# Two token tiles in a bank of PSUM: the output products of the GLUs and of layer 1's heads, added to the residual in one operation per pair

## The chip, the cores and the metric

The kernel runs on one core of a Trainium2 chip, as one program in one launch. A core has engines with instruction queues of their own: TensorE for matmuls (PE in the profile; PEld is its loading of weights), VectorE (DVE), ScalarE (ACT), GpSimd (POOL), and SyncE (SP), which here only issues DMAs. They wait for one another through semaphores. SBUF is the working memory of 128 partitions; PSUM holds results of matmuls. The metric is the device time of one execution in microseconds, the median of several runs.

## The reference

A residual stream x of 2048 tokens (4 sequences of 512) by 256 columns in fp32 goes through four layers. In each, a mixer and a feed-forward part read the same layernorm of x, and both are added to x:

```python
xn = layernorm(x)                  # before each layer
x = x + mixer(xn) + ffn(xn)

# the gated linear unit (GLU), in all four layers' feed-forward parts
y = (silu(xn @ w_gate) * (xn @ w_up)) @ w_down

# layer 0: mixer = Mamba2, 32 heads of 64, state 128, causal convolution of 4; ffn = GLU(1024)
# layer 1: mixer = latent attention, 16 heads, causal, rotary; ffn = GLU(1024) + 8 of 512 product-key experts
out = softmax(mask(qf @ kf.T * scale)) @ v          # per head
mixer = out.reshape(b, s, 16 * 128) @ wo
# layer 2: mixer = attention over heads within a token; ffn = top 2 of 8 experts (width 128) + a shared GLU(256)
# layer 3: mixer = causal attention, 16 heads of 128;   ffn = top-p weighted GLUs of 8 experts (width 512)
```

What the change touches is the last product of a GLU and of layer 1's heads, and the addition of these products to x.

## The kernel before

x lives in SBUF as `c.x`: 128 partitions by 16 token tiles by 256 columns (`DM`), four tiles (`TPB`) to a sequence, four sequences (`NB`). The normalized x stands transposed in `c.xnT`. Weights arrive in units by DMA.

**PSUM** has eight banks of 512 fp32 columns, given out by `c.ps(tag)`: four of tag "mm", two of "tr", two of "acc". A tile of a tag takes the bank whose last reader has finished. "tr" serves transposes above all, "acc" sums of output products.

**A GLU** (`glu_pieces`, L163-L211) takes a unit of weights and goes through the sequences. For each of its `n` column blocks of 128 it makes gate and up projections for 512 tokens (L134, in `project`), the activation (`sg`, L195, or `silu_times`) and their product hT (L196). Then, tile by tile, it multiplies the hT blocks by the output weights: `n` matmuls (L203) into the first half of a bank, 256 columns; `add_scaled` (L147) adds that half bank to x with one VectorE instruction, `tensor_add` at L151, or with a factor per token (layer 3's experts) `scalar_tensor_tensor` at L152. Layer 0's GLU and a quarter of layer 1's (the first of two units, for sequences 0 and 1) run beside Mamba, with output in "tr" banks and five hT buffers; the remaining layer 1 pieces run beside the heads and product-key experts in "acc" banks. Layer 2's shared GLU has two blocks of 128, layer 1's and layer 0's units have four.

**Layer 1's heads** (`latent_pieces`) go through 4 groups of 4 heads, 4 sequences and 2 pairs of heads. Scores (L631) become probabilities (L634 on VectorE, exponent on ScalarE), are transposed (L812, "tr"), and multiplied with the compressed values (L856, "acc") into `zT` (L862). After the second pair, the output products of the four token tiles follow at L869: two matmuls to a half bank of "acc", added to x by `add_scaled`. Queries with the rotary part come from L787 to L789 (`psw`, `qf`) and from L899 and L902 (`qT`). Layer 3's heads have their own output loop (`heads_out`, L647), which calls `add_scaled` too.

**Order of work.** Each of these functions is a generator; `weave` (L214) runs several together. After each `yield` the stream that is least far along by its share of cost goes on, and the number yielded is what it has then spent. `weave` also counts down `c.later`: the transposes of a sequence's layernorm wait for eight such steps, or until a stream needs that sequence (`c.settle`). `c.part_done(b)` says that one contribution to a sequence of x is complete, and starts the next layernorm with the last one. From this program order a scheduler makes the queue of each engine; it can move an instruction ahead where its buffers and inputs allow, unless `keep_in_program_order` pins it. [...]

**Mamba** (layer 0) projects, convolves (L268, `xc` at L272), transposes `xc` (L415, "tr") into `xdt` (L417), makes decays by a scan (L409, POOL L435) and state updates (`S`, L464 to L470), adds the partial `y` (POOL L458, VectorE L479), and multiplies it with the output weights group by group (L495, "tr"); each product is copied to or added to `acc` in SBUF (ScalarE L499, VectorE L501), which frees the bank, and `acc` goes to x at L514.

**Layer 2's experts** sort the tokens into slots per half of the sequences. `dispatch` (router scores L1290, `chosen` L1275, positions `at` L1340, normalized weights `tot` L1374) gives `ids`; `gather` (L1383) fetches the rows of each slot from the normalized x in DRAM by an indirect DMA, issued by POOL, two tiles to a pair of slots, into `xs`: three buffers for the first half of the sequences, one for each pair for the second. Then `experts` goes through the pairs: transposes (`turn`, L1401), projections (`hidden`, L1413; hs at L1421), transposes (`turn_hidden`, L1427), output (`down`, L1435, copied at L1440). Beside it runs `head_mix`, whose projections are at L142 and L1171, with `prod` on POOL at L1188 and the addition to x on VectorE at L1193.

```python
weave(c, (shared, 41.0, 0.0), (dispatch(), 34.0, 0.0), flush=False)
weave(
    c, (experts[0], 40.0, 0.0), (mix(), 12.0, 0.0),
    (last.gather(xs, len(PAIRS), every), 12.0, 0.0), flush=False,
)
```

Of the kernel before, what the change touches and what calls it, by code (L numbers as in the profile page):

```python
# [15 lines left out]
P = 128  # L16
NB, SEQ, DM = 4, 512, 256
NT = NB * SEQ
NTILE = NT // P
TPB = SEQ // P  # L20
# [62 lines left out]
def v3(ap, b):  # L83
    return ap.rearrange("p (a b) -> p a b", b=b)
# [46 lines left out]
def project(c, out, w, cols, tokens):  # L131

    for d in range(2):
        c.nc.tensor.matmul(  # L134
            out, lhsT=w[:, d, cols], rhs=c.xnT[:, d, tokens], start=(d == 0), stop=(d == 1)
        )
# [10 lines left out]
def add_scaled(c, t, part, w=None):  # L147

    x = c.x[:, t, :]
    if w is None:  # L150
        return c.nc.vector.tensor_add(x, part, x)  # L151
    return c.nc.vector.scalar_tensor_tensor(x, part, w, x, ALU.mult, ALU.add)  # L152


def silu_times(c, pool, out, gate, other):


    sg = c.tile(pool, [P, SEQ], "sg", bufs=2)
    c.nc.scalar.activation(sg, gate, AF.Tanh, scale=0.5)
    c.nc.vector.scalar_tensor_tensor(sg, sg, 1.0, gate, ALU.add, ALU.mult)  # L160
    c.nc.vector.scalar_tensor_tensor(out, sg, 0.5, other, ALU.mult, ALU.mult)


def glu_pieces(
    c, pool, srcs, n=4, width=512, split=1, factor=None, tanh=False, bufs=8, out_tag="acc",
    last=True, first=0, loaded=False, seqs=range(NB),
):

    nc = c.nc
    per = n // split
    for u, src in enumerate(srcs, first):
        w = src if loaded else c.unit(src)
        wg = v3(w[:, : 2 * width], width)
        wu = v3(w[:, 2 * width : 4 * width], width)
        wd = v3(w[:, 4 * width : 4 * width + n * DM], DM)
        for b in seqs:  # L180
            tokens = slice(b * SEQ, (b + 1) * SEQ)
            c.settle(b)
            hT = []
            for k in range(n):
                cols = slice(k * P, (k + 1) * P)
                pg, pu = c.ps(), c.ps()
                project(c, pg, wg, cols, tokens)
                project(c, pu, wu, cols, tokens)
                h = c.tile(pool, [P, SEQ], "hT", bufs=bufs)
                hT.append(h)  # L190
                if tanh:
                    silu_times(c, pool, h, pg, pu)
                else:
                    sg = c.tile(pool, [P, SEQ], "sg", bufs=2)
                    nc.scalar.activation(sg, pg, AF.Silu)  # L195
                    nc.vector.tensor_mul(h, sg, pu)  # L196
                yield 3.4
            for t in range(TPB):
                for s in range(split):
                    po = c.ps(out_tag)[:, :DM]  # L200
                    for i in range(per):
                        k = s * per + i
                        nc.tensor.matmul(  # L203
                            po, lhsT=hT[k][:, t * P : (t + 1) * P], rhs=wd[:, k, :],
                            start=(i == 0), stop=(i == per - 1),
                        )
                    tt = b * TPB + t
                    add_scaled(c, tt, po, factor(u * split + s, tt) if factor else None)
                if last and u == first + len(srcs) - 1 and t == TPB - 1:
                    c.part_done(b)  # L210
                yield 0.43 * n  # L211


def weave(c, *streams, flush=True):  # L214
# [442 lines left out]
def latent_pieces(c, a, keep, prep, open_pool):  # L657
# [4 lines left out]
    nc, tc = c.nc, c.tc  # L662
# [13 lines left out]
    with prep as pre:  # L676
# [3 lines left out]
        for b in range(NB):  # L680
# [3 lines left out]
            for t in range(TPB):  # L684
                tt = b * TPB + t
# [98 lines left out]
    def rotate(pes, psw, qf):  # L784
        pec = c.tile(pool, [P, SEQ], "pec", bufs=1)
        nc.vector.tensor_mul(pec, pes, cosq)
        tc.keep_in_program_order(nc.vector.tensor_mul(psw, psw, sinq))  # L787
        nc.vector.tensor_add(qf[:KL, 1, :], pec[:KL, :], psw[:KL, :])
        nc.vector.tensor_add(qf[KL:, 0, :], pec[KL:, :], psw[KL:, :])  # L789

    def probabilities(s, i):
        p, h = s // 2, s % 2
        b = p // 2 % 4
        if i == 0:
            totals[s] = c.tile(pool, [P, TPB], "total")
        rinv = totals[s]
        prs[s].append(exp_scores(
            c, pool, late, qfs[p][:, h, :], kf[:, h, b * SEQ : (b + 1) * SEQ], i, rinv[:, i : i + 1]
        ))
        if i >= TPB - 2:  # L800

            done = slice(0, i + 1) if i < TPB - 1 else slice(i, i + 1)
            nc.vector.reciprocal(rinv[:, done], rinv[:, done])
            for j in range(TPB)[done]:
                nc.scalar.mul(prs[s][j], prs[s][j], rinv[:, j : j + 1])  # L805

    def turned(s, j):

        pt = c.ps("tr")
        n = SEQ - j * P  # L810
        for i in range(j, TPB):
            nc.tensor.transpose(  # L812
                pt[:, (i - j) * P : (i - j + 1) * P], prs[s][i][:, j * P : (j + 1) * P], c.ident
            )
        copy = nc.scalar.copy if j % 2 else nc.vector.tensor_copy
        return lambda: copy(PTs[s][:, START[j] : START[j] + n], pt[:, :n])

    START = (0, 512, 896, 1152)
    qfs, prs, totals, PTs, zTs = {}, {}, {}, {}, {}
# [3 lines left out]
    for s in range(65):  # L823
        if s < 64:
            prs[s] = []
        for i in range(TPB):
            if s < 64:
                probabilities(s, i)
            if s > 0:
                if i == 0:  # L830
                    PTs[s - 1] = c.tile(pool, [P, 1280], "PT")
                ready, copy = copy, turned(s - 1, i)
                if ready:
                    ready()
            if i == 0 and s % 2 == 1 and s < 63:
                rotate(*turning)
            yield 0.85
            if i == 1 and s % 2 == 0 and s < 62:
                turning = queries(s // 2 + 1)
                yield 2.6  # L840
        if copy:
            copy()
            copy = None
        if s > 0:
            del prs[s - 1]
        if s % 2 == 1:
            continue
        if s == 0:
            continue

        p = s // 2 - 1
        g, b, pair = p // 8, p // 2 % 4, p % 2
        z = c.ps("acc")
        for j in range(TPB):
            for h in range(2):
                tc.keep_in_program_order(nc.tensor.matmul(  # L856
                    z[h * KL : (h + 1) * KL, j * P :], lhsT=cv[:, b * TPB + j, :],
                    rhs=PTs[s - 2 + h][:, START[j] : START[j] + SEQ - j * P],
                    start=(j == 0), stop=(j == TPB - 1),
                ))  # L860
        zTs[pair] = c.tile(pool, [P, SEQ], "zT", bufs=3)
        nc.scalar.copy(zTs[pair], z)  # L862
        yield 2.1
        if pair == 1:
            wz = weights[g][4]
            for t in range(TPB):
                po = c.ps("acc")[:, :DM]
                for k in range(2):
                    nc.tensor.matmul(  # L869
                        po, lhsT=zTs[k][:, t * P : (t + 1) * P], rhs=wz[:, k, :],  # L870
                        start=(k == 0), stop=(k == 1),
                    )
                add_scaled(c, b * TPB + t, po)
                if g == 3 and t == TPB - 1:
                    c.part_done(b)
                yield 0.85


def product_key_pieces(c, a, keep, pool, dram, xn):
# [901 lines left out]
```

## Time and profile before

| what | value |
|---|---|
| median of 3 runs (lowest to highest) | 3194.76 us (3190.83 to 3198.62) |
| the profiled execution | 3179.26 us |
| its span in the trace | 3177.5 us |
| granted TensorE clock, mean | 0.992 |
| DMA packets moved | 185.16 MB, mean 58 GB/s |

The profiled execution is one run, with the time of each instruction. Its own time lies 1.8 us above its span, and 15.5 us below the median of the timed runs. The page gives for each engine its busy time, its share of the span and its number of instructions. In the rows of groups stand line, engine, operation, output and inputs, shape and number; then busy time and mean duration in ns; then the idle time of the engine just ahead of them, with what ended most of it. The waits list, for one engine, which line waited for which tile of which engine, the total in us, how often, and the longest. A line of the timeline has start and duration in us, engine, line, operation, and in brackets the idle time before it with its releaser. The layers follow one another: layer 0 runs to about 903 us of the span, layer 1 to 1530, layer 2 to 1800, layer 3 to the end, with some work of a layer beside the end of the one before it.

### The profile page before, as it was taken

What the parts mean: (1) busy time and instruction counts of PE and PEld (TensorE: products, weight loads), DVE (VectorE), ACT (ScalarE), POOL (GpSimd) and SP (SyncE); (2) the same over time, 40 slices, a digit from 0 to 9 for tenths busy, and PEclk for the clock granted to TensorE, in tenths of its full rate; (3) what the DMA queues carried; (4) which work ended last, traced back from release to release, by engine and by line L of the source; (5) the groups of instructions that cost most, each with busy time, mean ns of one, the idle gap of its engine ahead of it and who ended that gap; (6) DMA issues with size and microseconds to landing.
All of it is one profiled execution on the core that took longest, in us unless ns stands there. A gap on an engine that the chain in (4) does not pass through costs nothing.

```text
span 3177.5 us, 35877 instructions
## 1 busy us (share of the span) xinstructions
PE 3081.6 (97%) x12502; PEld 1879.8 (59%) x12502; DVE 1851.9 (58%) x4786; ACT 1257.6 (40%) x2908; POOL 640.0 (20%) x525
## 2 busy tenths in 40 slices
PE   8999999999899999999989999999999999999999
PEld 5566566565555555555566566566666665555555
DVE  5777778777677777887646654554554522222222
ACT  4434435444356666667424433333333401111111
POOL 0464545555400122331053000000000000000000
PEclk9999999999899999999999999999999999999999
DMA  4233233232310244344143000000000000000000
GB/s 130 77 103 119 93 95 110 89 117 83 110 36 25 68 98 116 103 112 142 47 113 110 7 21 7 1 27 1 21 1 1 20 20 20 20 20 20 0 0 27
DMA packets 89091, 185.16 MB, mean 58 GB/s; under 512 B 14192, under 2 KB 57216, under 8 KB 84176
## 3 DMA queue, kind: packets, MB, share of 16 engines
q1 hardware_dynamic: 74448, 135.05, 13.1%
q0 software_dynamic: 14176, 47.01, 6.1%
q8 instruction: 99, 1.62, 0.2%
q10 hardware_dynamic: 288, 0.82, 0.1%
q14 instruction: 80, 0.66, 0.1%
HBM read 160.95 MB, written 12.98 MB: 55 GB/s over the span
## 4 chain that ended last, share of the span: by engine, by line
PE 78%; DVE 10%; DMA 4%; POOL 3%; ACT 2%; issue 2%; SPq 1%; DVEq 0%; ACTq 0%; POOLq 0%
PE mm L134 31%; PE acc L203 8%; PE mm L631 7%; PE mm L142 5%; PE acc L1102 4%; PE acc L647 3%; DMA G<-own 2%; PE tr L1094 2%; PE tr L495 2%; DVE G L409 2%; DVE cy L268 2%; PE tr L812 2%; PE acc L856 1%; PE acc L869 1%; DMA psw<-pes 1%
## 5 line engine op out<-in xcount | busy, mean ns | idle before, releaser
L134 PE MATMUL mm<-xnT,wu 128*128 128x512 f32 x2128 | 955.6, 596 | 2.3 <-ACT sg L195 0.7
L134 PEld LDWEIGHTS mm<-xnT,wu 128*128 128x128 f32 x2128 | 398.4, 191 | 461.3 <-issue 430.8
L638 ACT ACTIVATE pr<-pr,nm 128x128 f32<-128x128 f32 (+3 forms) x512 | 285.9, 559 | 294.3 <-DVE nm L634 292.8
L195 ACT ACTIVATE sg<-mm 128x512 f32<-128x512 f32 x176 | 104.6, 594 | 607.0 <-PE mm L134 606.9
L196 DVE TENSOR_TENSOR hT<-sg,mm 128x512 f32<-128x512 f32 x176 | 120.4, 684 | 380.7 <-PE mm L134 369.0
L634 DVE CUSTOM_DVE_ANT_0 pr<-mm,late 128x128 f32<-128x128 f32 (+3 forms) x512 | 245.0, 482 | 88.3 <-PE mm L631 82.4
L203 PE MATMUL acc<-wu,hT 128*128 128x256 f32 x1280 | 290.9, 380 | 0.7 <-DVE x L151 0.4
L203 PEld LDWEIGHTS acc<-wu,hT 128*128 128x128 f32 x1280 | 240.0, 190 | 51.3 <-issue 19.2
L134 PE MATMUL mm<-xnT,w_in 128*128 128x512 f32 x512 | 231.1, 596 | 0.4 <-DVE hT L196 0.4
L973 POOL DMA_INDIRECT e<-in_p_experts,ids x128 | 128.4, 1003 | 451.7 <-DVE x L152 366.0
L409 DVE TENSOR_TENSOR_SCAN G<-G,eye 128x1024 f32<-128x1024 f32 x64 | 157.0, 2453 | 52.3 <-DMA G<-own 51.8
L631 PE MATMUL mm<-kf,qf 128*128 128x128 f32 (+3 forms) x512 | 179.1, 446 | 7.9 <-DVE qf L789 5.7
L435 POOL TENSOR_TENSOR G<-G,CB 128x1024 f32<-128x1024 f32 x64 | 151.8, 2372 | 162.0 <-DVE G L409 80.5
L268 DVE SCALAR_TENSOR_TENSOR cy<-mm,ws,cy 128x511 f32<-128x511 f32 (+2 forms) x216 | 158.7, 741 | 41.4 <-ACT cy L264 37.8
L631 PE MATMUL mm<-k,q 128*128 128x128 f32 (+3 forms) x512 | 176.6, 435 | 1.1 <-DVE q L1067 1.1
L421 ACT ACTIVATE xD<-xc,ws 128x128 f32<-128x128 f32 x256 | 84.8, 391 | 203.9 <-POOL y L458 191.6
L134 PEld LDWEIGHTS mm<-xnT,w_in 128*128 128x128 f32 x512 | 97.1, 192 | 101.3 <-issue 94.3
L152 DVE SCALAR_TENSOR_TENSOR x<-acc,cw,x 128x256 f32<-128x256 f32 x128 | 61.9, 483 | 155.5 <-PE acc L203 155.5
L1102 PE MATMUL acc<-PT,V 128*128 128x512 f32 (+3 forms) x512 | 149.5, 433 | 0.0
L1067 DVE TENSOR_SCALAR q<-mm,bias 128x512 f32<-128x512 f32 x64 | 48.0, 750 | 169.1 <-PE mm L134 169.1
L151 DVE TENSOR_TENSOR x<-acc,x 128x256 f32<-128x256 f32 x168 | 70.5, 421 | 118.4 <-PE acc L647 98.4
L812 PEld LDWEIGHTS tr<-con,pr 128*128 128x128 f32 x640 | 81.7, 143 | 90.2 <-ACT pr L805 28.8
(308 smaller groups left out, 5017.8 us busy)
## 6 DMA issues: line engine op xcount, KB each, us to landing
G<-own SPq DMA_DIRECT2D x64, 512.0 KB, 4.3
w_in<-in_m_units SPq DMA_DIRECT2D x16, 1024.0 KB, 5.2
eb<-since SPq DMA_DIRECT2D x96, 128.0 KB, 3.2
wu<-in_o_units SPq DMA_DIRECT2D x8, 1536.0 KB, 6.5
wo<-in_m_units SPq DMA_DIRECT2D x16, 512.0 KB, 3.8
psw<-pes SPq DMA_DIRECT2D x128, 64.0 KB, 2.6
wu<-in_g_units SPq DMA_DIRECT2D x4, 1536.0 KB, 6.8
wu<-in_f_units SPq DMA_DIRECT2D x4, 1536.0 KB, 6.9
```

The source lines that it names most:

```text
L134: c.nc.tensor.matmul(out, lhsT=w[:, d, cols], rhs=c.xnT[:, d, tokens], start=(d == 0), stop=(d == 1))
L142: c.nc.tensor.matmul(out, lhsT=c.xnT[:, d, tokens], rhs=w[:, d, cols], start=(d == 0), stop=(d == 1))
L203: nc.tensor.matmul(po, lhsT=hT[k][:, t * P : (t + 1) * P], rhs=wd[:, k, :], start=(i == 0), stop=(i == per - 1),)
L268: nc.vector.scalar_tensor_tensor(y[:, j:], src[:, : SEQ - j], conv[:, k, 3 - j : 4 - j], y[:, j:], ALU.mult, ALU.add,)
L409: nc.vector.tensor_tensor_scan(flat, flat, eye.rearrange("p h t -> p (h t)"), 0.0, ALU.mult, ALU.add)
L435: nc.gpsimd.tensor_mul(G, G, seqs[b][2][:, t, :][:, None, :].to_broadcast([P, HG, P]))
L631: nc.tensor.matmul(sc, lhsT=q[:, i * P : n], rhs=k[:, :n], start=True, stop=True)
L634: nc.vector.tensor_tensor_reduce(out=pr, in0=sc, in1=late[:, SEQ - n :], scale=1.0, scalar=-NEG, op0=ALU.add, op1=ALU.min, accum_out=nm,)
L638: nc.scalar.activation(pr, pr, AF.Exp, bias=nm, scale=-1.0, accum_out=total)
L812: nc.tensor.transpose(pt[:, (i - j) * P : (i - j + 1) * P], prs[s][i][:, j * P : (j + 1) * P], c.ident)
L973: nc.gpsimd.indirect_dma_start(out=e, out_offset=None, in_=a["p_experts"], in_offset=bass.IndirectOffsetOnAxis(ap=ids[:, t, k : k + 1], ax ...
L1102: nc.tensor.matmul(z[:, j * P :], lhsT=head["V"][:, j, h, :], rhs=head["PT"][:, j, j * P :], start=(j == 0), stop=(j == TPB - 1),)
```

## The change

A new function `add_pair` adds 512 columns, two neighbouring token tiles, to x in one `tensor_add`. `glu_pieces` without a factor now takes two tiles at a time: 2 x `n` matmuls fill the two halves of one bank, one addition follows, and the yield carries the cost of both tiles. With a factor (layer 3's experts) it goes tile by tile as before. The output loop of layer 1's heads does the same, with 4 matmuls to a bank. Layer 3's heads keep `add_scaled`. The matmuls themselves, their shapes and number, are the same.

```diff
+def add_pair(c, t, parts):
+
+    x = c.x[:, t : t + 2, :]
+    c.nc.vector.tensor_add(x, parts, x)
...
-            for t in range(TPB):
+
+            step = 1 if factor else 2
+            for t in range(0, TPB, step):
                 for s in range(split):
-                    po = c.ps(out_tag)[:, :DM]
-                    for i in range(per):
-                        k = s * per + i
-                        nc.tensor.matmul(
-                            po, lhsT=hT[k][:, t * P : (t + 1) * P], rhs=wd[:, k, :],
-                            start=(i == 0), stop=(i == per - 1),
-                        )
+                    po = v3(c.ps(out_tag)[:, : step * DM], DM)
+                    for j in range(step):
+                        for i in range(per):
+                            k = s * per + i
+                            nc.tensor.matmul(
+                                po[:, j, :], lhsT=hT[k][:, (t + j) * P : (t + j + 1) * P],
+                                rhs=wd[:, k, :], start=(i == 0), stop=(i == per - 1),
+                            )
                     tt = b * TPB + t
-                    add_scaled(c, tt, po, factor(u * split + s, tt) if factor else None)
-                if last and u == first + len(srcs) - 1 and t == TPB - 1:
+                    if factor:
+                        add_scaled(c, tt, po[:, 0, :], factor(u * split + s, tt))
+                    else:
+                        add_pair(c, tt, po)
+                if last and u == first + len(srcs) - 1 and t == TPB - step:
                     c.part_done(b)
-                yield 0.43 * n
+                yield 0.43 * n * step
...
-            for t in range(TPB):
-                po = c.ps("acc")[:, :DM]
-                for k in range(2):
-                    nc.tensor.matmul(
-                        po, lhsT=zTs[k][:, t * P : (t + 1) * P], rhs=wz[:, k, :],
-                        start=(k == 0), stop=(k == 1),
-                    )
-                add_scaled(c, b * TPB + t, po)
-                if g == 3 and t == TPB - 1:
+            for t in range(0, TPB, 2):
+                po = v3(c.ps("acc"), DM)
+                for j in range(2):
+                    for k in range(2):
+                        nc.tensor.matmul(
+                            po[:, j, :], lhsT=zTs[k][:, (t + j) * P : (t + j + 1) * P],
+                            rhs=wz[:, k, :], start=(k == 0), stop=(k == 1),
+                        )
+                add_pair(c, b * TPB + t, po)
+                if g == 3 and t == TPB - 2:
                     c.part_done(b)
-                yield 0.85
+                yield 1.7
```

## The prediction, made before any run of the changed kernel

> **What bounds the kernel now.** I read first the page's busy times, then a table of four stages (the four layers, cut where their first projections begin), then what PE waited for, then the rows of the touched operations.
>
> ```profile
> PE 3081.6 (97%) x12502; PEld 1879.8 (59%) x12502; DVE 1851.9 (58%) x4786; ACT 1257.6 (40%) x2908; POOL 640.0 (20%) x525
> 0.00:903.00 903.00, 854.40 (x3971) 531.49 (x3972) 674.05 (x1003) 395.15 (x837) 419.61 (x305) 0.99 0.32 101
> 903.00:1530.00 627.00, 603.67 (x2634) 344.68 (x2635) 483.77 (x1693) 407.83 (x1086) 121.72 (x122) 0.99 0.34 89
> 1530.00:1800.00 270.00, 249.34 (x1130) 175.58 (x1127) 167.97 (x521) 107.36 (x217) 87.06 (x82) 0.97 0.26 75
> 1800.00:3178.00 1378.00, 1374.24 (x4773) 828.02 (x4770) 526.10 (x1569) 347.26 (x770) 11.62 (x16) 1.00 0.04 13
> ```
>
> The stage lines give length, then busy us of PE, PEld, DVE, ACT and POOL, granted clock, DMA share, GB/s. PE is the bound everywhere: its idle time is 48.6, 23.3, 20.7 and 3.8 us, 96 us in all. DVE is busy 75% of layer 0 and 77% of layer 1, so a shorter DVE queue pays only where PE waits for it. Those waits (line waited for, us in total, times, longest):
>
> ```profile
> PE tr L1401 <- DMA xs<-xn_half,ids: 11.7, 1, 11.7
> PE tr L415 <- DVE x L151: 6.1, 6, 3.7
> PE acc L869 <- DVE x L151: 3.6, 1, 3.6
> PE tr L495 <- DVE x L151: 3.3, 3, 1.7
> PE tr L203 <- DVE acc L501: 2.7, 2, 2.1
> PE mm L1290 <- DVE chosen L1275: 2.5, 1, 2.5
> PE tr L495 <- DVE acc L501: 2.3, 2, 2.0
> PE acc L203 <- DVE x L151: 0.4, 1, 0.4
> ```
>
> L151 is the addition that the change pairs; PE waits 13.4 us for it (6.1 + 3.6 + 3.3 + 0.4), always to get a PSUM bank back. L501 frees the same two "tr" banks: 5.5 us more (2.7 + 2.3, and 0.5 at L415, not shown). The rows of the operations:
>
> ```profile
> L151 DVE TENSOR_TENSOR x<-acc,x 128x256 f32<-128x256 f32 x168 | 70.5, 421 | 118.4 <-PE acc L647 98.4 <-PE acc L203 11.2 <-PE acc L869 8.1
> L151 DVE TENSOR_TENSOR x<-tr,x 128x256 f32<-128x256 f32 x40 | 16.6, 414 | 4.3 <-PE tr L203 4.3
> L470 DVE TENSOR_TENSOR S<-mm,S 128x512 f32<-128x512 f32 x32 | 22.1, 690 | 3.2 <-PE mm L464 0.4
> ```
>
> The last is what the change makes: a 128x512 fp32 addition of PSUM to SBUF. The others add half as much.
>
> [...] a pair fills it with separate 256-column matmuls, so the bank count stays and each matmul keeps its 380 ns row. [...] 5-us windows after stalls of 3.72, 3.30 and 11.66 us show granted clocks of 0.71, 0.50 and 0.50. After the longest, one group of four transposes takes 1.20 us where 0.60 is usual. I price a slow phase at 1.8 us[...].
>
> **The change, part by part.**
>
> *DVE.* Of the 208 L151 additions, 144 pair up: 40 on tr (32 of layer 0's GLU, 8 of layer 1's), 64 of layer 1's heads (L869) and 24 of its GLU on acc, 16 of layer 2's shared GLU. 144 x 0.421 = 60.6 us become 72 x 0.690 = 49.7 us: 11 us less, on an engine that isn't the bound, hence nothing directly. Layer 3's 64 heads additions and its expert GLU (L152) keep their form.
>
> *PE.* The same matmuls, nothing direct. But the order of the built instructions changes: 60 groups of four L203 matmuls become 30 groups of eight. A bank is held for 8 matmuls, and one is needed half as often. I counted in PE's order how much matmul work, by trace durations, lies between the last matmul into a bank and the first of its next use. On tr, reuses with under 1.8 us of cover fall from 15 to 4; those of L415 after L203, which carry the 3.72 us stall, from 6 to 0. On acc, 15 reuses of L869 after L869 with under 1 us don't exist any more. Layer 3's order is unchanged.
>
> *Layer 0.* The tr waits that can go: 6.1 + 3.3 + 5.5 = 14.9 us, plus 1.8 of slow clock = 16.7. Their cause is often DVE's queue: before the 3.72 us stall, the addition sat behind y (L479), which waited for POOL. A PE that gets past the bank meets the next result of the same queue. Bounds: all kept, -16.7; none, 0. I take rather under half, -7.
>
> *Layer 1.* L869's 3.57 us came from an addition behind psw (L787), which waited 4.89 us for a DMA. With 3.6 + 0.4 and a slow phase, 5.8 us can go; closeness of probabilities to their transposes (L812) also improves, with under 1 us of cover 11 times before and 3 after. Against that, L902's eight matmuls stand 0.35 us nearer to qT on average (2.8 us if all surface) and one L203 directly follows its hT (at most some 1.5 us). From -7 to +4; I take -4.
>
> *Layer 2.* The 16 additions of the shared GLU fall where the queues of a gather decide. Before, POOL's order is the first half's gathers for pairs 0 to 3 (of expert slots), all 23 of the second half, then pairs 4 to 7, then prod (L1188). Each takes 1.25 us. PE stalls at pair 4:
>
> ```profile
> 1631.47 1.20 PE L1401 MATMUL tr<-con,xs 128*128 128x128 f32 x4 [11.66 <-DMA xs<-xn_half,ids]
> 1637.42 1.94 POOL L1188 TENSOR_TENSOR prod<-s,qkv 128x1024 f32<-128x1024 f32 x1
> 1639.39 1.22 DVE L1193 TENSOR_TENSOR x<-x,prod 128x1024 f32<-128x1024 f32 x1 [3.96 <-POOL prod L1188]
> 1641.40 0.38 PE L1427 MATMUL tr<-con,hs 128*128 128x128 f32 x2
> ```
>
> After, L1401's transposes of pairs 0 to 2 stand ahead of the last L203 groups, so their buffers come free earlier and gathers of pairs 4 and 5 go ahead of the 23. Pair 4's stall goes. Late next is prod, still behind 23 + 4 gathers on POOL; L1193 waits for it, and on DVE the hs of pair 4 stands behind L1193. The 23 start at 1596.2 instead of 1598.3, since ids come some 2 us earlier (the 2.5 us wait for chosen is covered by moved work), end at 1625, two more pairs' gathers at 1630, prod at 1632, L1193 at 1633.3, hs at 1633.7. PE, without its stall and that wait, is there at about 1624.7 and waits 9 us. The pair-4 transpose at 1641.4 comes at about 1633.8: 7.6 us gained, less some 2 us for a slow clock that now follows. I take -5. Bounds: -14 if prod slips in between the gathers and no new stall forms (11.7 + 2.5), +1 if the new one costs as much as the old ones. POOL's descriptor queue is where I trust the arithmetic least: gathers took 3.2 us in the median from issue to landing[...].
>
> *Larger pieces.* A yield hands over to another stream: two tiles are now one piece of 8 x 0.38 = 3.0 us before another stream has its turn, and layernorm's transposes, due after eight steps, come later by work. Price 0 where the table of covers is right.
>
> Sum: -7 - 4 - 5 + 0 = -16 us on the profiled execution's 3179.26 us (span 3177.5 and 1.8 around it): 3163. The shown median is 15.5 us above that execution; shifted by the same 16, it becomes **3179 us**, 0.995 of before.
>
> **Rivals.**
>
> *No change.* Waits only move: in layers 0 and 1 the next DVE result is late by as much, and prod's wait takes the whole place of the gather's. For it: layer 0's DVE is itself chained to POOL and to DMA. Against: the covers of data, not only of banks, are equal or better. It gives -3 to 0: 3193.
>
> *More.* All bank waits go (16.7 + 5.8) and layer 2 keeps its 5: -27.5, 3167. For it: DVE is also relieved of 11 us of work, most of it in these two layers. Against: PE's idle time in layers 0 and 1 is 72 us, most of it with other causes; a PE that is early meets these.
>
> *Slower.* Lumps starve the chains that the output tiles filled. The covered waits sit in Mamba's scan and in the heads; each was filled by single 1.5 us groups, and now every second filler is missing there. 64 pairs lie in layers 0 to 2 outside the shared GLU; if a third of them each cost one missing filler of 1.5 us, that is 21 x 1.5 = +32 us, with the -16: +16, 3211. It decides once more than eleven pairs lose one filler each. Against: in the built order other streams' work has moved into those gaps.
>
> **How the numbers follow.** Chances: forecast 0.52, more 0.16, no change 0.17, slower 0.15. A measurement tells about 0.2% from none, 6.4 us. The forecast's own range is 3172 to 3188, of which nearly all is faster; "more" reaches to 3163, slower up to 3215. From 3164 to 3196 holds about eight in ten: it leaves out most of "slower". Faster: 0.16 + 0.52 with little taken off, plus a little of "no change": 0.69. Same: 0.16. Slower: 0.15.
>
> **What would show it.** Right: L151 left with 64 instructions; 72 additions of 128x512 at about 0.69 us; PE waits for "x" on tr and acc under 5 us in all; the second stage's idle about 4 us less and the first's about 7; no wait at L1401 for xs near 1620, but one of about 9 us at L1427 or what feeds it, with prod as its end; layer 3 within 1 us. Wrong: new waits of PE, each 1 to 2 us, in layers 0 and 1 for xc, xdt, hT, PT or qf, which would be the starving; a granted clock below 0.99 there; or an idle sum in layer 2 above 21 us.

## The result, and the profile after

| | before | changed |
|---|---|---|
| median of 22 runs each, us | 3191.36 | 3182.81 |
| lowest to highest | 3181.78 to 3200.39 | 3170.12 to 3192.93 |
| ratio, 95% interval | | 0.9972 (0.9962 to 0.9983) |
| the profiled execution | 3179.26 | 3176.93 |

The change gains 0.28%, 8.5 us by the medians, where 16 were forecast. The two profiled executions lie only 2.3 us apart, since that of before was faster than all 22 timed runs of its kernel (12.1 us below their median; that of the changed kernel 5.9 below). One run of a later experiment took 5384.6 us at a granted clock of 0.554; the ratios leave it out. The page's line of busy times and the four stages of the changed kernel:

```profile
PE 3091.7 (97%) x12502; PEld 1890.4 (60%) x12502; DVE 1847.0 (58%) x4714; ACT 1259.5 (40%) x2910; POOL 636.4 (20%) x525
0.00:903.00 903.00, 858.39 (x3993) 537.57 (x3994) 677.72 (x991) 395.64 (x839) 415.95 (x305) 0.98 0.32 101
903.00:1530.00 627.00, 610.39 (x2678) 350.17 (x2677) 479.43 (x1659) 412.36 (x1098) 121.40 (x122) 0.99 0.33 88
1530.00:1800.00 270.00, 251.07 (x1072) 175.98 (x1071) 164.78 (x498) 104.35 (x204) 87.40 (x82) 0.94 0.26 75
1800.00:3175.00 1375.00, 1371.90 (x4764) 826.71 (x4762) 525.06 (x1567) 347.18 (x770) 11.61 (x16) 1.00 0.04 13
```

PE is busy 10.1 us longer (3091.7 against 3081.6) with the same 12502 instructions, and the granted clock of the third stage fell from 0.97 to 0.94. PE idles 12.4 us less (83.5 against 95.9 us), and matmuls at a slower clock take most of that back. To see where, one needs marks that are the same work in both kernels: the first and last scores matmul of layer 1's heads, and the first of layer 3's. The lines of one source in each kernel (before first), with first and last start:

```profile
L631 PE MATMUL mm<-kf,qf x512: 272/486/634, 909.9 to 1524.0; 128*128 128x128 f32 x43, 128*128 128x256 f32 x43, 128*128 128x512 f32 x43, 128*128 128x384 f32 x42
L631 PE MATMUL mm<-k,q x512: 272/474/676, 1727.3 to 2531.6; 128*128 128x128 f32 x43, 128*128 128x256 f32 x43, 128*128 128x512 f32 x43, 128*128 128x384 f32 x42
```

```profile
L643 PE MATMUL mm<-kf,qf x512: 272/484/697, 902.2 to 1513.0; 128*128 128x128 f32 x43, 128*128 128x256 f32 x43, 128*128 128x512 f32 x43, 128*128 128x384 f32 x42
L643 PE MATMUL mm<-k,q x512: 272/474/676, 1725.2 to 2529.4; 128*128 128x128 f32 x43, 128*128 128x256 f32 x43, 128*128 128x512 f32 x43, 128*128 128x384 f32 x42
```

Layer 0, to the first mark, became 7.7 us shorter, layer 1's heads 3.3 (610.8 against 614.1). From there to layer 3 it takes 212.2 us instead of 203.3: layer 2 lost 8.9 of these 11. Layer 3 is unchanged (1450.2 us before and 1450.0 after, to the end of the span).

The rows of the additions in the changed kernel, and PE's waits that answer to those shown of before:

```profile
L158 DVE TENSOR_TENSOR x<-acc,x 128x512 f32<-128x512 f32 x52 | 35.8, 688 | 29.9 <-PE acc L212 20.6 <-PE acc L882 9.1
L151 DVE TENSOR_TENSOR x<-acc,x 128x256 f32<-128x256 f32 x64 | 27.1, 424 | 98.3 <-PE acc L659 98.3
L158 DVE TENSOR_TENSOR x<-tr,x 128x512 f32<-128x512 f32 x20 | 13.5, 676 | 0.0
```

```profile
PE mm L1426 <- DVE qkv L1184: 7.1, 1, 7.1
PE tr L427 <- DVE x L158: 6.8, 2, 3.6
PE tr L507 <- DVE x L158: 4.0, 2, 2.1
PE tr L507 <- DVE acc L513: 3.6, 3, 1.9
PE mm L1360 <- DVE at L1353: 3.0, 2, 1.6
```

There are 72 additions of 49.3 us together. PE waits for x only on tr now, four times instead of nine, but longer: 10.8 us against 9.4 there. The wait for xs of 11.7 us is gone, and L1426 waits 7.1 us in its place. The timeline of POOL, VectorE and PE there (start, duration, engine, line; in brackets the wait and its end):

```profile
1632.85 1.94 POOL L1201 TENSOR_TENSOR prod<-s,qkv 128x1024 f32<-128x1024 f32 x1
1634.83 1.23 DVE L1206 TENSOR_TENSOR x<-x,prod 128x1024 f32<-128x1024 f32 x1 [10.92 <-POOL prod L1201]
1635.97 0.45 DVE L1184 TENSOR_TENSOR qkv<-mm,h_small 128x288 f32<-128x288 f32 x1
1636.57 3.75 PE L1426 MATMUL mm<-weights,xsT 128*128 x8 [7.13 <-DVE qkv L1184]
```

POOL makes prod only after its gathers, L1206 waits for prod, L1184 stands behind L1206 on VectorE, though the matmuls it reads (L142) had ended by 1629.2 and VectorE was idle up to 1634.8, and it is the one that frees the mm bank that PE wants. The eight matmuls after the wait take 3.75 us, where 1.89 is usual: the granted clock is 0.50 there (1636.5 to 1641.5).

### The profile page after: what moved, and what is told of

Its sections match the earlier page's. It is cut to its first block, busy times and chain, and to the rows that moved or that the text cites. A ratio compares the mean times of both kernels' runs of the same rounds, so it can differ in the third digit from the quotient of the medians.

```text
span 3175.2 us, 35804 instructions
## 1 busy us (share of the span) xinstructions
PE 3091.7 (97%) x12502; PEld 1890.4 (60%) x12502; DVE 1847.0 (58%) x4714; ACT 1259.5 (40%) x2910; POOL 636.4 (20%) x525
## 4 chain that ended last, share of the span: by engine, by line
PE 80%; DVE 10%; DMA 4%; ACT 2%; POOL 2%; issue 1%; SPq 1%; DVEq 0%; ACTq 0%; POOLq 0%
PE mm L134 31%; PE acc L212 8%; PE mm L643 7%; PE mm L142 5%; PE acc L1115 4%; PE acc L659 3%; DMA G<-own 3%; PE tr L1107 2%; PE tr L507 2%; DVE G L421 2%; PE tr L824 2%; PE acc L868 2%; DVE cy L280 2%; PE acc L486 1%; PE tr L212 1%
## 5 line engine op out<-in xcount | busy, mean ns | idle before, releaser
L134 PE MATMUL mm<-xnT,wu 128*128 128x512 f32 x2128 | 960.3, 598 | 2.9 <-DVE cy L280 1.3
L134 PEld LDWEIGHTS mm<-xnT,wu 128*128 128x128 f32 x2128 | 400.4, 191 | 464.5 <-issue 434.9
L202 DVE TENSOR_TENSOR hT<-sg,mm 128x512 f32<-128x512 f32 x176 | 120.5, 685 | 385.8 <-PE mm L134 369.8
L134 PE MATMUL mm<-xnT,w_in 128*128 128x512 f32 x512 | 230.9, 597 | 0.0
L421 DVE TENSOR_TENSOR_SCAN G<-G,eye 128x1024 f32<-128x1024 f32 x64 | 158.3, 2474 | 66.9 <-DMA G<-own 66.8
L134 PEld LDWEIGHTS mm<-xnT,w_in 128*128 128x128 f32 x512 | 97.6, 192 | 103.4 <-issue 97.8
L507 PE MATMUL tr<-wo,y 128*128 128x256 f32 x512 | 126.7, 391 | 7.9 <-DVE x L158 4.0
```

The source lines that it names most:

```text
L134: c.nc.tensor.matmul(out, lhsT=w[:, d, cols], rhs=c.xnT[:, d, tokens], start=(d == 0), stop=(d == 1))
L421: nc.vector.tensor_tensor_scan(flat, flat, eye.rearrange("p h t -> p (h t)"), 0.0, ALU.mult, ALU.add)
L507: nc.tensor.matmul(po, lhsT=y[:, k, :], rhs=groups[i][1][:, k, :], start=(k == 0), stop=(k == 3))
```

## The experiments

Twelve experiments ran in three groups, each on one chip beside the kernel before. These were three chips; the median of before was 3190.6 us on the first, 3218.4 and 3218.1 on the others, so times are compared by ratio, and times within a trace only on one chip. Which chip the runs of the result had is not on record; their median of before, 3191.4 us, is that of the first. "Ids apart" is the time from the first half's ids in layer 2 to the second half's: the length of a dispatch. In the executions of the result it is 29.8 us before and 39.5 after.

| kernel | chip | ratio to before, 95% | ids apart, us |
|---|---|---|---|
| pairs in layer 2 only | 1 | 1.0009 (0.9997 to 1.0021) | 37.7 |
| all pairs but layer 2's | 1 | 0.9956 (0.9944 to 0.9968) | 29.8 |
| two additions on a shared bank | 1 | 0.9977 (0.9959 to 0.9996) | 39.0 |
| larger yields alone | 1 | 1.0013 (1.0002 to 1.0025) | 38.3 |
| pairs, a yield for each tile | 2 | 0.9990 (0.9976 to 1.0004) | 39.2 |
| changed, prod on VectorE | 2 | 0.9972 (0.9959 to 0.9986) | 39.6 |
| all pairs but layer 2's, gathers first | 2 | 1.0037 (1.0021 to 1.0053) | 48.6 |
| pairs on tr only | 2 | 0.9963 (0.9949 to 0.9976) | 32.8 |
| changed, again | 3 | 0.9980 (0.9969 to 0.9990) | 36.8 |
| all pairs but layer 2's, again | 3 | 0.9981 (0.9972 to 0.9991) | 33.8 |
| changed, router 64 wide | 3 | 0.9982 (0.9971 to 0.9993) | 33.3 |
| changed, router 128 wide | 3 | 1.0008 (0.9995 to 1.0021) | 39.0 |

### Layer 2 alone, and all but layer 2

My theory was that layer 2 gains by the moved gathers, and that what it lost in the profiled execution was chance. The rival: pairs there lengthen the dispatch. In `glu_pieces`, the first kernel's edit (with the heads' loop of before) and the second's:

```diff
-            step = 1 if factor else 2
+            step = 2 if n == 2 else 1
...
-            step = 1 if factor else 2
+            step = 2 if not factor and n == 4 else 1
```

> Only layer 2's shared GLU adds by pairs; the order of the other layers is that of the kernel before. Theory A (the pairs in layer 2 move the first half's gathers ahead, so the 11.7 us wait of PE for xs goes and a wait of about 7 us for prod takes its place; what layer 2 lost in the profiled execution was slow clock by chance): no wait of PE for xs over 2 us, one of 6 to 9 us that ends with qkv or hs behind prod, time 3 to 6 us below the kernel before. Theory B (the pairs' longer groups hold up layer 2's dispatch, so what is gained at the gathers is lost there): the same waits, but ids of the second half come at least 5 us later counted from the first chosen matmul than before (47.8 us there), and the time is within 2 us of the kernel before or above it. Layers 0 and 1 as before: first chosen matmul within 3 us of 1550.

> All pairs but those of layer 2's shared GLU; layers 0 and 1 have the order of the changed kernel, layer 2 that of before. Theory A: layers 0 and 1 carry about 8 to 11 us of gain, so the first chosen matmul comes at 1539 to 1543, layer 2 keeps its 11.7 us wait for xs, and the time is 7 to 11 us below before. Theory B: the same layers gain and layer 2 costs nothing, so this is faster than the changed kernel by 3 to 8 us, 11 to 15 below before. If the gain of layers 0 and 1 in the profiled execution was clock alone: first chosen matmul near 1550 and time as before.

With pairs in layer 2 alone the time didn't fall (at best by 0.03%). The wait for xs went and one of 7.2 us for qkv came, as both theories had it, and the ids came 37.7 us apart. With all pairs but those, the time fell by 0.44% (14.0 us; 10.2 to 17.9), more than the whole change gave, the wait for xs was 11.6 us and the ids were 29.8 apart. The rival holds on this chip; the kernel with two additions below, which has the time of the changed one, had a median of 3182.8 us in the same group, against 3176.4. The marks of layers 0 and 1 were later than expected (908.8 and 1524.5). Of this, 5.7 us were there at the first pair already (its addition starts at 46.9 us, in the changed kernel at 41.2). They are slow matmuls at the start: the same 14 thin ones (L142, at 14.2 and 14.1 us) take 3.04 us in one and 1.65 in the other, and two of L134 take 2.06 us up to some 25.7 us in the one and 1.08 to 1.11 behind it, where in the other they take 2.05 before 14 us and 1.02 to 1.10 after. Layer 0 then agrees with the changed kernel (908.8 - 5.7 = 903.1); its heads took 615.7 us, so that layer 1's 3.3 us are within what one execution differs from another.

What makes a dispatch longer is seen in windows from the first ids to the second: before, then changed (columns as in the stage lines):

```profile
1568.00:1598.00 30.00, 27.53 (x136) 19.40 (x136) 20.99 (x85) 5.44 (x9) 7.77 (x8) 1.00 0.13 36
```

```profile
1559.00:1599.00 40.00, 35.10 (x141) 25.12 (x141) 21.22 (x82) 8.64 (x12) 11.88 (x12) 0.82 0.14 40
```

The window is 10 us longer; PE's idle time grew from 2.5 to 4.9 us, and its busy time from 27.5 to 35.1 with nearly the same matmuls, at a mean clock of 0.82 instead of 1.00. That is about 0.18 x 40 = 7.2 us of clock and 2.4 us of waits. PE's work in that stretch, cut:

```profile
1562.99 2.71 PE L142 MATMUL mm<-t_small,xnT 128*128 128x8 f32 x16
1565.56 5.74 PE L212 MATMUL acc<-wu,hT 128*128 128x256 f32 x14
1575.77 1.13 PE L212 MATMUL acc<-wu,hT 128*128 128x256 f32 x4 [1.03 <-DVE hT L202]
1579.85 0.43 PE L1303 MATMUL mm<-chosen,con 128*128 128x64 f32 x2 [2.07 <-DVE chosen L1288]
1580.12 3.02 PE L134 MATMUL mm<-xnT,wu 128*128 128x512 f32 x4
1590.99 2.19 PE L1360 MATMUL mm<-hit,at 128*128 128x23 f32 x16 [1.39 <-DVE at L1353]
```

The second block of router matmuls (L142) before, and in another execution of the changed kernel (on the third chip, see below):

```profile
1573.14 1.85 PE L142 MATMUL mm<-t_small,xnT 128*128 128x8 f32 x16
1574.85 1.97 PE L203 MATMUL acc<-wu,hT 128*128 128x256 f32 x8
```

```profile
1587.82 1.85 PE L142 MATMUL mm<-t_small,xnT 128*128 128x8 f32 x16
1589.52 3.27 PE L212 MATMUL acc<-wu,hT 128*128 128x256 f32 x14
```

No wait reaches 3 us, and the first slow stretch has no wait ahead of it at all: PE works without a gap from 1550 us on, yet the 16 router matmuls of 8 columns take 2.71 us instead of 1.85 and the 14 products behind them 5.74 instead of 3.27. From 1563.7 to 1570.5 the granted clock is 0.50 with PE busy throughout. Two more slow stretches, at 0.50 from 1580.8 to 1584.2 and from 1594.5 to 1601.3, come after the waits of 2.07 and 1.39 us; in the first of these, four matmuls of L134 take 3.02 us where 1.96 is usual.

Pairs of the shared GLU hand the filling work over in larger pieces. In PE's order two of its products stand between the two blocks of router matmuls, where eight stood before; 14 follow the second block instead of eight, and fewer are left for the wait for `at`. The slow stretch without a wait is there in four of the six traces with two products between the blocks (the second block took 2.71 us in the changed kernel, and on the third chip, without it, 1.85), and in none of the eight with eight (1.85 before). Thin matmuls nearly side by side thus go with it, but not each time; why is not shown.

### Bank, addition, or handing over?

```diff
# two additions on a shared bank, from the changed kernel
-    c.nc.vector.tensor_add(x, parts, x)
+    for j in range(2):
+        add_scaled(c, t + j, parts[:, j, :])
# larger yields alone, from the kernel before: GLU without factor, and heads
-                yield 0.43 * n
+                if factor:
+                    yield 0.43 * n
+                elif t % 2:
+                    yield 0.86 * n
...
-                yield 0.85
+                if t % 2:
+                    yield 1.7
# pairs, a yield for each tile, from the changed kernel, in both loops over j
+                        if step == 2 and j == 0:
+                            yield 0.43 * n
...
-                yield 0.43 * n * step
+                yield 0.43 * n
```

> The changed kernel with two additions of 128x256 on the shared bank in place of one of 128x512: VectorE has its 11 us back, the bank and the handing over by pairs stay. If the gain comes from the bank and the order (my theory): time within 3 us of the changed kernel, 5 to 9 below before. If it comes from VectorE's shorter queue: half or more of the gain is gone, within 4 us of before. PE's waits for x on tr and acc tell: below 13.4 us in the first case, above it in the second.

> The kernel before with half-bank tiles and its additions of 256, but work handed over to the other streams after two tiles instead of one. If the gain comes from a bank that serves two tiles: no gain here, and PE waits for x at least as much as before (13.4 us), since two tiles in a row want two banks; time within 3 us of before or up to 10 above. If it comes from the order that the larger yields make: the time is 5 to 9 us below before, as the changed kernel's.

> The changed kernel with its full banks and additions by pairs, but a yield after each token tile, so that other streams get their turn as often as before. If the larger pieces starve layer 2's dispatch (theory B): the second half's ids come 29 to 33 us after the first half's (29.8 before, 39.5 in the changed kernel), the 7 us wait behind prod stays, and the time is 5 to 10 us below the changed kernel's, 12 to 18 below before, if layers 0 and 1 keep their gain. If the bank or the addition does it: ids 38 to 40 us apart and a time as the changed kernel's.

With two additions the kernel has the time of the changed one (0.9977; 1.3 to 13.1 us below before) and its marks (902.7 and 1514.1), and PE waits 9.9 us for x. So VectorE's shorter queue isn't what gains, as far as this interval tells. Larger yields alone made it slower by 0.13%, with the first mark at 919.9. The waits of this kernel:

```profile
PE tr L418 <- DVE x L151: 12.3, 7, 2.7
PE tr L498 <- DVE x L151: 5.8, 5, 2.1
PE mm L1417 <- DVE qkv L1175: 4.7, 1, 4.7
```

With a bank for each tile, two tiles in a row made PE wait 18.1 us on tr, twice as much as before. Larger pieces need the shared bank. But the bank isn't enough: with shared banks and a yield after each tile, PE's waits for x on tr are the lowest of all (4.4 us),

```profile
PE tr L429 <- DVE acc L515: 5.2, 3, 3.1
PE tr L429 <- DVE x L158: 2.8, 3, 1.8
PE tr L509 <- DVE x L158: 1.6, 1, 1.6
```

and still it isn't measurably faster than before (0.9990). Its first mark is at 920.2, where the changed order (with prod on VectorE) had 911.2 on that chip, both with the late start of 5.7 us; pairs on tr alone had 907.4 without it. Other waits stand in the place of those for x: 7.9 us for acc (5.5 before) and 3.0 for xdt (0.4 at L495 before). The expectation for this kernel was wrong twice: layer 0 lost its gain, and ids stayed 39.2 us apart. So smaller yields don't mend the dispatch; both the larger yields without the bank and the bank without the larger yields make it long.

### Pairs on tr only

```diff
-            step = 1 if factor else 2
+            step = 2 if out_tag == "tr" else 1
```

with the heads' loop of before.

> Pairs only where the output goes to tr: layer 0's GLU and the quarter of layer 1's that runs beside it. By my prediction this half of the gain is -7 us of the -11 in layers 0 and 1: 5 to 9 us below before, layer 1's 3.6 us wait of L869 for x still there. If layer 1's heads carry it instead: within 3 us of before.

It took 0.37% off (11.9 us; 7.7 to 16.4), more than the 5 to 9 expected. The wait for x that was to stay in layer 1's heads was only 0.3 us here. The gain is most of what all pairs but layer 2's gave on the first chip (0.44%). The heads' pairs therefore seem to carry little: on this chip the heads took 626.0 us from first to last scores matmul without them, and 631.7 and 630.3 in the two kernels that have them with larger yields; on the first chip 610.8 to 615.7 with them and 614.1 and 616.5 without. Runs on two chips don't settle more.

### The wait behind prod, and the gathers

```diff
# changed, prod on VectorE; the kernel with gathers first has this too
-    nc.gpsimd.tensor_mul(
+    (nc.vector if b == 0 else nc.gpsimd).tensor_mul(
         prod, s[:, :, :, None]
...
# all pairs but layer 2's, gathers first
-                for half, more in ((first, first.gather(xs, 3, every)), (last, None))
+                for half, more in ((first, first.gather(xs, 12, every)), (last, None))
```

> The changed kernel, with prod of the first sequence in layer 2 made by VectorE instead of POOL; PE's order is the same. If prod behind POOL's gathers is what PE waits for at 1629 (my theory): the 7.1 us wait for qkv is gone, no other wait over 3 us takes its place in layer 2, and the time is 6 to 9 us below the changed kernel's. If the gathers of the next pairs are as late: a wait for xs of 4 us or more takes its place and the gain is under 3 us. The ids stay 38 to 40 us apart in both cases.

> All pairs but the shared GLU's, a buffer for each pair of the first half's gathers (12 instead of 3) so that they stand ahead of the second half's on POOL, and prod of the first sequence on VectorE. By the theory that POOL's queue alone makes layer 2's long wait: the 11.6 us wait for xs goes and none over 3 us comes in layer 2, the slow clock after it goes too, and the time is 9 to 14 us below the kernel with all pairs but the shared GLU's, 22 to 28 below before. If what follows is as late (combine, the second half's experts): less than half of that.

Neither did what was expected. With prod on VectorE the wait for qkv at L1426 went, and one of 10.4 us at L1440 came. These ran on the second chip, where something else ends layer 2's long wait, as the third chip shows more plainly. ScalarE and PE in the kernel with all pairs but layer 2's, on the first chip and then on the third, at the same place of the program:

```profile
1607.48 1.99 PE L1426 MATMUL mm<-weights,xsT 128*128 x8
1609.51 0.38 ACT L1433 ACTIVATE gate<-mm 128x256 f32<-128x256 f32 x1 [7.85 <-PE mm L1426]
1610.59 1.08 ACT L1419 COPY xsT<-tr 128x512 f32<-128x512 f32 x2 [0.70 <-PE tr L1414]
```

```profile
1624.42 1.99 PE L1426 MATMUL mm<-weights,xsT 128*128 x8
1637.11 0.38 ACT L1433 ACTIVATE gate<-mm 128x256 f32<-128x256 f32 x1 [18.51 <-remote]
1647.66 0.58 ACT L1419 COPY xsT<-tr 128x512 f32<-128x512 f32 x1 [10.17 <-remote]
1648.30 3.49 PE L1426 MATMUL mm<-weights,xsT 128*128 x8 [20.37 <-ACT xsT L1419]
```

On the first chip, ScalarE takes `gate` 0.04 us after the eight matmuls end. On the third it takes it 10.7 us after, while POOL issues its row of gathers, and the next copy another 10 us later; what ended these waits the profile can't name ("remote"). PE then waits 20.4 us. On the second chip ScalarE waited up to 21.7 us in this way in the changed kernel with prod on VectorE, so that the removal of the wait behind prod had nothing to show, and its ratio (0.9972) is that of the changed kernel on the first chip. With all 24 gathers of the first half in a row, a stop of this kind fell into the dispatch: VectorE stood for 7.4 us at L202, its end again "remote", PE waited 13.7 us, and the ids came 48.6 us apart. This kernel was slower than before by 0.37%. Whether either edit helps on a chip like the first was not tried.

### The changed kernel again, and a router of other width

```diff
# the router of layer 2: 64 (or 128) columns for each tile, the first 8 read
-        project_tokens(
-            c, pl[:, t * E : (t + 1) * E], wr, slice(0, E), slice(tt * P, (tt + 1) * P)
-        )
+        for d in range(2):
+            nc.tensor.matmul(
+                pl[:, t * W : (t + 1) * W], lhsT=c.xnT[:, d, tt * P : (tt + 1) * P],
+                rhs=wide[:, d * E : d * E + W], start=(d == 0), stop=(d == 1),
+            )
...
-    nc.vector.tensor_copy(p, v3(pl, E))
+    nc.vector.tensor_copy(p, v3(pl, W)[:, :, :E])
```

> The changed kernel once more, on the same chip as the three others. If the slow dispatch of layer 2 belongs to the change and not to one execution: the second half's ids again come 38 to 41 us after the first half's, with 5 us or more of slow clock between them, and from the last scores matmul of layer 1's heads to the first of layer 3's it is 5 us or more longer than before (203.3 us there on the first chip). If it was chance: 30 to 33 us.

> All pairs but those of layer 2's shared GLU once more, beside the changed kernel. If pairing the shared GLU costs: 4 to 8 us below the changed kernel, ids 30 to 33 us apart. If the earlier difference was noise: within 2 us of it.

> The changed kernel, with layer 2's router scores computed 64 columns wide instead of 8 (the extra columns aren't read). In the built order, eight output products of the shared GLU stand between the two blocks of router matmuls again, as before the change, instead of two; POOL's order of gathers is that of the changed kernel. If the dispatch's order is what layer 2 loses by: ids 30 to 34 us apart, under 3 us of slow clock between them, 5 to 9 us below the changed kernel. If pairs in the shared GLU cost by themselves: ids 38 us or more apart, time as the changed kernel or above.

> The same with 128 columns: more work in each router matmul, eight output products between the blocks again, and POOL's gathers as in the kernel before (first half's pairs 0 to 3 ahead of the second half). If the dispatch's order decides: ids 30 to 35 us apart, little slow clock, and the 11.7 us wait for xs in place of the 7 us behind prod, so 2 to 6 us below the changed kernel. If not: ids 38 us or more apart and time as the changed kernel or above.

On this chip the changed kernel gains 0.20% and the one without pairs in layer 2 0.19%: no difference, against 4 to 8 us expected. The dispatch is longer with the pairs here too (36.8 against 33.8 us, though less than the 38 to 41 expected), but behind it stands ScalarE's stop: PE waits 11.8 us for hs in the changed kernel and 20.4 us for xsT in the other. From the last scores matmul of layer 1 to the first of layer 3 both take as long, 222.3 and 221.0 us. The router of 64 columns shortened the dispatch to 33.3 us, as the theory of its order said, and PE then waited 20.9 us for xsT; no time was gained. The edit widens the matmuls and moves the products at once, so it doesn't tell which of the two shortened the dispatch. The router of 128 columns fits neither theory: the ids are 39.0 us apart, although eight products stand between the blocks and the stretch without a wait is not slow there. Its slow stretches follow waits of 2.5 us for chosen and 2.6 for `at`, and the clock from ids to ids is 0.79, as low as in any of these traces. What in the order makes a dispatch slow is therefore not settled; that it costs clock as well as waits is.

## Why the prediction came out as it did

The time lay in the range and the direction was right; the forecast of -16 us was nearly twice what was measured. That 3179 us missed by only 3.8 is luck in part: the three runs of before that it started from had a median 3.4 us above that of the 22. By its steps:

- **VectorE's 11 us, hence nothing directly.** Right: 72 additions took 49.3 us (49.7 forecast), and with two additions on the bank no difference in time was seen.
- **Bank waits.** "PE waits for x on tr and acc under 5 us in all" was wrong. On acc they went (3.6 and 0.4 us, none after); on tr 9.4 us became 10.8. The cover between two uses of a bank was counted in matmul work, but the addition comes when VectorE's queue lets it: ahead of the wait of 3.2 us that ends at 802.7, it stood behind a scan (L421) of 4.4 us. (By the list of additions, 64 groups of four matmuls become 32 of eight, not 60 and 30; no term of the sum rests on it.)
- **Layer 0, -7.** It was -7.7, and this stands in more than one execution: with the late start taken off, the changed order reached the first mark at 902.2, 902.7 and 903.1 us on the first chip, the order of before at 909.9 and 910.2. But the reason is another than the one given, and the size was a guess ("rather under half"), so that it was met is luck; the 1.8 us for a slow phase, in its sum and in layer 1's, were an estimate that the windows given with it don't show. The waits for x on tr didn't shrink, and the kernel with the fewest of them gained nothing. Some waits of PE that aren't for x went or shrank in the order of the larger pieces (from 90 to 785 us, those for sg at L464, 2.6 us, and for acc of L499, 1.6, went; those for xc fell from 3.3 to 2.4). They don't add up to 7.7, so where all of it comes from stays open.
- **"Larger pieces. Price 0."** The step that failed. In layer 0 the larger pieces gain, together with the shared bank (either alone gained nothing measurable, the one on the first chip, the other on the second); in layer 2, on the first chip, they cost.
- **Layer 1, -4.** -3.3 in the profiled execution; the wait of L869 for x is gone as forecast. Other executions with the same order gave 611.4 and 615.7 us on that chip, the order of before 614.1 and 616.5: a gain of this size isn't shown.
- **Layer 2, -5.** It was +8.9 in the profiled execution. The trade of waits came as worked out, with the end at L1426 (L1413 of before) and qkv instead of the next step and hs: 7.1 us behind prod (about 9 forecast) for 11.7 at the gathers, and a slow clock after it (0.50 from 1636.5 to 1641.5). The term that failed was "ids come some 2 us earlier": from the first ids to the second took 9.7 us more, 7.2 of it clock. I priced a slow clock only behind waits as long as the three given, 3.30 to 11.66 us. In this trace it came with less: none of the dispatch's waits reached 3 us, and the first slow stretch (0.50 from 1563.7 to 1570.5) had no wait ahead of it. Whether the thin matmuls or the short waits bring it on was not shown. The wait was also nearer to the given figures than forecast: 1641.4 less the two waits named, 11.7 and 2.5, is 1627.2 and not 1624.7, which makes it 6.5 us.
- **Layer 3, 0.** Right: 0.2 us.
- **The signs.** The idle time of the first stage fell by 4.0 us (about 7 named) and that of the second by 6.7 (about 4 named), though the fixed cuts move work between the stages. The granted clock of the first stage was 0.98, below the 0.99 that was named as a sign of being wrong; PE's idle time in the third was 18.9 us, below the 21 named.

So the layers before came to -11.0 in the profiled execution, as forecast (-7 and -4) but not by the forecast's mechanism, and layer 2 took most of it back. The "slower" rival had a mechanism that fits in part, in the wrong place: it looked for missing fillers in Mamba and the heads, where the change gains, and left out the shared GLU.

The best version on the first chip is the one with pairs everywhere but in layer 2's shared GLU, 0.44% below before; on the third it has the time of the changed kernel.

## What to carry to other kernels

Where several streams share an engine's queue, the size of a piece can decide as much as its cost: here two results in one bank paid only together with larger pieces (0.9972 of before with both, 0.9990 and 1.0013 with one of the two), and the same larger pieces lengthened a serial chain of short steps (39.5 us against 29.8). Mark the same work in both traces before believing a gain by stage: in the two profiled executions 11 us were won and 9 lost out of sight of the total. Look at the granted clock in stretches of thin matmuls and short waits (0.82 on average from ids to ids here), not only behind a long wait, and try a change on more than one chip before its parts are ranked.

## What the runs showed of the hardware

- Time went with the granted clock from run to run. In the 22 runs of the changed kernel, the mean clock lay between 0.986 and 0.993, and the time correlated with it at -0.86, at 3.1 us for 0.001 (a straight line through the runs). By an estimate, matmuls that take as much longer as the clock is slower give about that: 0.001 of 3183 us is 3.2 us. The standard deviation of these runs is 7.0 us, so one profile of each kernel can't rank effects of that size.
- The granted clock was 0.50 with TensorE busy throughout from 1563.7 to 1570.5 us of the changed kernel, in the second of two blocks of 16 matmuls of 8 columns with two wider ones between them, and in the 14 wider ones behind it. In the clock records of the two profiled executions of the result, 22 stretches stand at 0.50: 14 of them last 3.41 us, six 6.83, one 10.24 and one 13.65; two more, of 0.36 and 2.33 us, are the last of their records.
- With the same instructions, ScalarE started at once on one chip and stopped for 18.5 us on another beside a row of indirect DMAs. The kernel before was 0.9% slower on the two chips where this was seen (3218 against 3191 us). What ScalarE waits for there stays open.
- The start of the kernel alone moved by 5.7 us between two executions with the same order, in one of which two matmuls of 512 columns took 2.06 us up to 25.7 us, in the other 2.05 only up to 14 and 1.02 to 1.10 after. Four of the fourteen traces have the late start (the first addition from tr at 46.9 to 47.5 us; in the others at 39.5 to 41.9).
